# A four-layer convolution and state-space network: every eighth product of the scan on GpSimd, convolutions in quarter tiles, projections as a third metered stream

## The chip, the core and the metric

The kernel runs on one core of one Trainium2 chip. Its time is the device time of one launch in microseconds, the median of several runs. The core's engines work side by side, each through its own list of instructions in order: TensorE (PE in the profile; PEld is its weight load), VectorE (DVE), ScalarE (ACT), GpSimd (POOL) and SyncE (SP), which issues the DMAs. They wait for one another by semaphores.

## The reference

The input `x` is 16 images of 192 channels of 32 x 32, all float32. Four layers follow one another, each as `x = x + layer(_gn(x))`, where `_gn` normalizes groups of channels. Layer 0 is a matrix-LSTM block with a 3x3 convolution and a normalization over the batch. Layer 1 is channel attention between depthwise 3x3 convolutions. Layer 2 is a selective scan in four directions over the 1024 pixels. Layer 3 mixes an image with shifted copies of itself. What matters here is layer 2 and the depthwise convolutions:

```python
def selective_scan(u, delta, A, Bs, Cs, Dskip):
    ...
    def step(h, xs_t):
        d_t, u_t, B_t, C_t = xs_t
        dA = jnp.exp(d_t[..., None] * A)
        h = h * dA + (d_t * u_t)[..., None] * B_t[:, :, None, :]
        y = jnp.einsum('bkdn,bkn->bkd', h, C_t)
        return (h, y)
    ...
xz = jnp.einsum('bchw,oc->bohw', x, in_proj_w)
xx, z = jnp.split(xz, 2, axis=1)
z1 = jax.nn.gelu(z, approximate=False)
xx = jax.lax.conv_general_dilated(xx, conv_w, (1, 1), 'SAME', feature_group_count=D_EXP, ...) + conv_b[None, :, None, None]
xx = jax.nn.gelu(xx, approximate=False)
...
x_dbl = jnp.einsum('bkdl,kcd->bkcl', xs, x_proj_w)
dts, Bs_, Cs_ = jnp.split(x_dbl, [R, R + N], axis=2)
dts = jnp.einsum('bkrl,kdr->bkdl', dts, dt_w)
delta = jax.nn.softplus(dts + dt_b[None, :, :, None])
```

There are 4 directions (K), 384 channels and 16 states (N) per channel, so an image has 4 x 384 x 16 recurrences of 1024 steps.

## The kernel before

**Stages.** `layer0` runs image by image and leaves its results in DRAM. The class `LayersB` does layers 1 to 3. For each image it has three parts. `prepare` (layer 1, and layer 2 up to the gated input `xx`) runs for the image after the one that is being scanned. `scans` does the recurrences. `complete` (the end of layer 2, and layer 3) runs for the image before. So in the long scan stage the scans of image b stand beside `prepare` of b+1 and `complete` of b-1.

**A unit.** A unit is 128 recurrences of 1024 steps: 16 channels by 8 states on the 128 partitions. An image has 192 units (`UNITS`), 48 per direction (`DIR_UNITS`). For unit u the engines do this:

- ScalarE, `decay(u)`: `h[u % 2] = exp(A * dl)`, written to PSUM (L1830).
- GpSimd, `inputs(u)`: `xs[u % 3] = du * bb` in SBUF (L1837), issued two units ahead.
- VectorE, `scan(u)`: one scan instruction in place in `h` (L1844).
- VectorE, `outputs(u)`: `hc[u % 3] = h * cb`, the product with C, written to SBUF (L1849).
- TensorE, `sums(u)`: four matmuls of 32 columns which add `hc` over the states into `acc` (L1882), issued one unit later. After every fourth unit `collect` copies `acc` to `y` on ScalarE (L1892).

SP loads `dl` (ring of two) and `du` (ring of three) for each two units, broadcast from DRAM (L1806), and `bb` and `cb` for each direction (L1800).

**The order by hand.** In the scan stage the order is written out by the program itself. `scans` walks over the units and keeps a model clock for each engine. `prepare` and `complete` are generators, wrapped as a `Stream`; a `yield "PE", 0` tells which engine the next piece uses. After the unit's own instructions `fits` decides whether the next piece of a stream may be issued now: the model clock of its engine must not be further than `OVER` beyond the end of the unit, and `ALLOW` limits what a unit may take on TensorE and VectorE. Costs are metered by `RATES` in `Metered`.

**Projections.** `front(k)` makes the step sizes of a direction: `project` and `steps` on TensorE, `keep`, `ends` and `logs` on ScalarE, `park` on GpSimd, which ends in two stores to DRAM (L1785, L1786). Its pieces have fixed units: `steps` at unit -18, -12, -6, 0, 6 and 12 of the direction, the rest one, two and four units later, whatever the clocks say.

**Convolutions.** `conv` does a depthwise 3x3 convolution on TensorE as nine matmuls with diagonal weights per half of the pixels, 18 in all, each over all channels of the tile (96 or 128). One PSUM bank of the stream holds the sum of a half, and one copy on ScalarE takes it out. `taps` loads the diagonals in three DMAs. For the first image VectorE computes the second half with nine multiply-adds. There are ten convolutions per image.

**PSUM.** `mm` hands out three banks: "bp" for `prepare`, "bc" for `complete`, "bf" for `front`.

**ScalarE's tables.** Exp and Ln lie in one table, Gelu in another. `ln_exp` loads the first explicitly, behind each Gelu and before each Ln; `has_ln` remembers whether it is there.

Most of the streams' instructions carry line L800, that of the metering helper.

Of the kernel before, what the change touches and what calls it, by code (L numbers as in the profile page):

```python
# [41 lines left out]
class Ctx:  # L42


    def __init__(self, tc, cpool, I):
        self.tc, self.nc, self.I = tc, tc.nc, I
        self.ordered = False
        self.has_ln = False
        nc = self.nc
        self.ident = cpool.tile([128, 128], F32, name="ident")  # L50
        nc.sync.dma_start(self.ident, I["c_ident"])
        self.blk6 = cpool.tile([P6, P6], F32, name="blk6")
        nc.sync.dma_start(self.blk6, I["c_blk6"])
        self.eps5 = cpool.tile([128, 1], F32, name="eps5")
        nc.vector.memset(self.eps5, 1e-5)
        self.one = cpool.tile([128, 1], F32, name="one")
        nc.vector.memset(self.one, 1.0)
        self.on192 = cpool.tile([P6, P6], F32, name="on192")
        nc.vector.memset(self.on192, 1.0 / C)
        self.on384 = cpool.tile([128, 128], F32, name="on384")  # L60
        nc.vector.memset(self.on384, 1.0 / INNER)
        self.ones = cpool.tile([128, 128], F32, name="ones")
        nc.vector.memset(self.ones, 1.0)

    def ln_exp(self):

        if self.ordered and self.has_ln:
            return
        self.has_ln = True
        if self.ordered:  # L70
            self.spent["ACT"] += TABLE
        i = self.nc.scalar.preload_act_table_set("natural_log_exp_and_others")
        if not self.ordered:
            self.tc.keep_in_program_order(i)
# [696 lines left out]
SLOT = 3.55  # L771
EARLY = 1.3
OWN = {"POOL": 2.36, "SUMS": 0.6, "START": 0.9, "DECAY": 1.1, "COLLECT": 0.57}
ENGINES = ("PE", "ACT", "POOL", "DVE")
ALLOW = {"PE": 2.7, "DVE": 0.3}
OVER = {"PE": 2.5, "ACT": 1.0, "POOL": 2.5}
LEAST = {"PE": 1.0, "ACT": 0.6, "POOL": 0.8}
# [3 lines left out]

class Metered:


    RATES = {"ACT": (0.07, 0.00105), "POOL": (0.1, 0.0022), "DVE": (0.08, 0.00105), "PE": (0.06, 0.0017)}
    LEAST = {"ACT": 0.2, "POOL": 0.2, "DVE": 0.12, "PE": 0.4}

# [3 lines left out]
    def __getattr__(self, op):  # L791
        f = getattr(self.engine, op)

        def issue(out, *args, **kw):
            base, each = self.RATES[self.name]
            self.spent[self.name] += max(self.LEAST[self.name], base + each * math.prod(out.shape[1:]))
            if op == "activation" and args[1] in (AF.Tanh, AF.Gelu):
                self.spent["ACT"] += TABLE * self.cx.has_ln
                self.cx.has_ln = False
            return f(out, *args, **kw)  # L800

        return issue
# [12 lines left out]
class Stream:  # L815
# [9 lines left out]
    def step(self):  # L825
        self.engine, lag, *mark = next(self.pieces, (None, 0))
        self.ready = self.at + lag
        self.piped = "piped" in mark

# [11 lines left out]
class LayersB:  # L841
# [10 lines left out]
    def mm(self):  # L852

        if self.bank is None:
            self.turn = (self.turn + 1) % 3
            tag = ("bp", "bc", "bf")[self.turn]
        else:
            tag = self.bank
        return self.mmp.tile([128, HL], F32, tag=tag, name="mm")

# [25 lines left out]
    def run(self):  # L886
        tc, NB = self.tc, self.NB
        self.bank, self.turn = None, 0
        with ExitStack() as ctx:
# [11 lines left out]
            self.parked = self.fetched = self.slots = self.scanned = self.read = 0  # L901

# [11 lines left out]
            with tc.manual_schedule():  # L914
                self.before, self.after = Stream(self.all(self.complete), "bc"), Stream(self.all(self.prepare), "bp")
                for b in range(NB):
# [6 lines left out]
    def setup(self):  # L923
# [3 lines left out]
        self.dqd = dp.tile([6, 128, 9, 128], F32, name="dqd")  # L927
        self.dvd = dp.tile([2, 2, P6, 9, P6], F32, name="dvd")
# [168 lines left out]
    def taps(self, p, src, w, first):  # L1097


        d = [self.slot("dg", [p, 3, p], "dg", 3) for _ in range(3)]  # L1100
        tv = None
# [3 lines left out]
        for t in range(3):  # L1105
            three = slice(3 * t, 3 * t + 3)
            if first:
                self.nc.vector.tensor_mul(
                    d[t], self.cx.ident[0:p, 0:p].unsqueeze(1).to_broadcast([p, 3, p]),
                    tv[:, three].unsqueeze(2).to_broadcast([p, 3, p]),  # L1110
                )
                self.nc.sync.dma_start(src[:, three, :], d[t])
            else:
                self.nc.sync.dma_start(d[t], src[:, three, :])
        return d, tv

    def conv(self, out, i, p, taps):


        nc = self.be  # L1120
        d, tv = taps
        for hf in range(2):
            if hf and tv is not None:
                yield "DVE", 0
                o = rows(out[:, half(hf)])
                for t in range(9):
                    v = self.pads[i][0:p, 16 + t // 3 : 32 + t // 3, t % 3 : t % 3 + W]
                    if t == 0:
                        nc.vector.tensor_scalar(o, v, tv[:, 0:1], None, op0=ALU.mult)
                    else:  # L1130
                        nc.vector.scalar_tensor_tensor(
                            o, v, tv[:, t : t + 1], o, op0=ALU.mult, op1=ALU.add
                        )
                continue
            yield "PE", 0
            ps = self.mm()[0:p, :]
            for t in range(9):
                if t in (2, 4, 6):
                    yield "PE", 0
                nc.tensor.matmul(  # L1140
                    ps, lhsT=d[t // 3][:, t % 3, :],
                    rhs=self.pads[i][0:p, 16 * hf + t // 3 : 16 * hf + t // 3 + 16, t % 3 : t % 3 + W],
                    start=(t == 0), stop=(t == 8),
                )
            yield "ACT", 0
            nc.scalar.copy(out[:, half(hf)], ps)

    def prepare(self, b):
# [193 lines left out]
        for g in range(3):  # L1342
            yield "ACT", 0
            nc.scalar.activation(xx[:, g, :], xg[:, g, :], AF.Gelu, bias=self.dw2b[:, g : g + 1])
        cx.ln_exp()
# [7 lines left out]
        for gs in ((0, 1), (2,)):  # L1353
# [10 lines left out]
            for g, z in zip(gs, zs):  # L1364
                yield "ACT", 0
                nc.scalar.activation(z, z, AF.Gelu)
                nc.sync.dma_start(self.zd[one(b), g].rearrange("o p l -> p (o l)"), z)
            cx.ln_exp()
# [5 lines left out]
    def complete(self, b):  # L1374
# [176 lines left out]
        for hf in range(2):  # L1551
# [57 lines left out]
            yield "ACT", 0  # L1609
            nc.scalar.activation(fin, fin, AF.Gelu)  # L1610
            cx.ln_exp()
# [22 lines left out]
    def scans(self, b, more, carry):  # L1634
# [4 lines left out]
        ahead = {}  # L1639
        for d in range(K + more):  # L1640
            for at, piece in self.front(d % K):
                if d % K or (at < 0) == (d > 0):
                    ahead.setdefault(d * DIR_UNITS + at, []).append(piece)
        for t in range(UNITS):
# [3 lines left out]
            for s in (self.before, self.after):  # L1648
                while s.engine == "ACT" and self.fits(s, now + EARLY - OVER["ACT"]):
                    self.advance(s)  # L1650
            if more or t + 1 < UNITS:
                self.decay((t + 1) % UNITS)
                clock["ACT"] += OWN["DECAY"]
# [4 lines left out]
            self.outputs(t)  # L1658
            clock["DVE"] += SLOT
            end = now + SLOT  # L1660
            if t > 0 or carry:
                self.sums((t - 1) % UNITS)
                self.collect((t - 1) % UNITS)
            self.fetch(t, more)
            self.bank = "bf"
            was = dict(self.spent)
            for piece in ahead.pop(t, ()):
                piece()
            for e in ENGINES:
                clock[e] += self.spent[e] - was[e]  # L1670
            for e in ALLOW:
                have[e] = min(have[e], 0.0) + ALLOW[e] - self.spent[e] + was[e]
            if more and t == FETCH:
                while self.parked < b + 2:
                    self.advance(self.after)
                self.fetch_xx()
            if t == UNITS - DIR_UNITS:
                while self.read < b:
                    self.advance(self.before)
            if t == 2:  # L1680
                self.scanned = b
            streams = (self.before, self.after)[:: 1 if t % 2 else -1]
# [6 lines left out]
        if not more:  # L1689
            while self.before.engine:  # L1690
                self.advance(self.before)
# [3 lines left out]
    def fits(self, s, end):  # L1695

        if not s.open(self.slots) or s.engine == "SP":
            return s.engine == "SP" and s.open(self.slots)
        at = self.clock[s.engine]
        if s.engine != "DVE":  # L1700
            end += OVER[s.engine]
        wait = s.inputs()
        if wait > at and (s.engine == "DVE" or wait + LEAST[s.engine] > end):
            return False
        return at < end + 0.1 and self.have.get(s.engine, 1.0) > 0.0

    def advance(self, stream):
        self.bank = stream.bank
        stream.at = self.slots
        was, wait = dict(self.spent), stream.inputs()  # L1710
        stream.step()
        for e in ENGINES:
# [7 lines left out]
    def begin(self):  # L1720

        for at, piece in self.front(0):
            if at < 0:
                piece()
# [12 lines left out]
    def front(self, k):  # L1737


# [48 lines left out]
        out = []  # L1788
        if k % 2 == 0:
            for hf in range(2):  # L1790
                at = -24 + 2 * hf
                out += [(at, lambda hf=hf: project(hf)), (at + 1, lambda hf=hf: keep(hf))]
        for n, at in enumerate((-18, -12, -6, 0, 6, 12)):
            for lag, f in ((0, steps), (1, ends), (2, logs), (4, park)):
                out.append((at + lag, lambda f=f, n=n: f(n // 2, n % 2)))
        return out
# [31 lines left out]
    def decay(self, u):  # L1828
        n, blk = divmod(u, BLOCKS)
        self.nc.scalar.activation(  # L1830
# [8 lines left out]
    def scan(self, u):  # L1839

        h, x = self.h[u % 2], self.xs[u % 3]
        if u // DIR_UNITS >= 2:
            h, x = h[:, ::-1], x[:, ::-1]
        self.nc.vector.tensor_tensor_scan(h, h, x, 0.0, op0=ALU.mult, op1=ALU.add)  # L1844
# [14 lines left out]
    def sums(self, u):  # L1859
# [5 lines left out]
        self.clock["PE"] += OWN["SUMS"]  # L1865
# [132 lines left out]
```

## Time and profile before

| | us |
|---|---|
| runs shown | 15191.56, 15242.16, 15250.05 |
| median | 15242.16 |
| profiled execution | 15228.48 |
| its span, first to last instruction | 15226.7 |

| engine | busy us | share of the span |
|---|---|---|
| TensorE | 12507.7 | 82% |
| VectorE | 12530.6 | 82% |
| ScalarE | 7798.3 | 51% |
| GpSimd | 10305.3 | 68% |

The shares are means over the whole span. The first scan starts at 3311.4 us and the last product ends at about 15091 us, so the scan stage has to be read by itself. In the profile a group of instructions shows its busy time, the mean of one in ns, and the engine's idle time before them with what ended it.

### The profile page before, as it was taken

The page shows a single profiled execution, that of the slowest core. Times are in us where ns is not written, and L with a number is a line of the kernel's source. Part 1 is how long each engine was busy: PE and PEld are TensorE (multiplying, and loading weights), DVE is VectorE, ACT ScalarE, POOL GpSimd, SP SyncE. Part 2 cuts the span into 40 slices and gives each one's busy share as a digit, 9 for nine tenths or more (in the row PEclk, how much of TensorE's full clock was granted, in tenths as well). Part 3 has the DMA queues.
Part 4 walks back from the last instruction along what each step waited for, and adds up shares of the span by engine and source line. Part 5 has one row for each costly group of instructions (what it writes and reads, how often), then busy time and mean ns, then how long its engine had stood idle before and what let it go on. Part 6 is the DMA issues. An engine that isn't in the chain of part 4 may idle for free. (4 is left out here: it accounts for less than half of the span.)

```text
span 15226.7 us, 183204 instructions
## 1 busy us (share of the span) xinstructions
PE 12507.7 (82%) x65856; PEld 4757.9 (31%) x65856; DVE 12530.6 (82%) x10115; ACT 7798.3 (51%) x10376; POOL 10305.3 (68%) x6314
## 2 busy tenths in 40 slices
PE   8999999978787778788887878788887888787655
PEld 4444444422232222222222222222222222222212
DVE  4444444459899999999999899999999999989997
ACT  3333333334555556465646565655555555555554
POOL 2222222227687878787878787878888787878785
PEclk9999999978888888888888888888888878888766
DMA  1000000047778787878777778777777787777775
GB/s 29 15 15 15 15 15 15 15 109 192 202 195 212 188 209 193 209 196 204 195 201 200 195 199 199 202 196 204 196 199 201 203 197 204 193 205 195 198 181 128
DMA packets 884772, 2412.01 MB, mean 158 GB/s; under 512 B 146672, under 2 KB 266944, under 8 KB 876224
## 3 DMA queue, kind: packets, MB, share of 16 engines
q1 hardware_dynamic: 871168, 2397.50, 62.2%
q8 instruction: 532, 8.72, 0.3%
q10 hardware_dynamic: 12736, 3.04, 0.1%
q14 instruction: 336, 2.75, 0.1%
HBM read 2019.10 MB, written 364.30 MB: 157 GB/s over the span
## 5 line engine op out<-in xcount | busy, mean ns | idle before, releaser
L1837 POOL TENSOR_TENSOR xs<-du,bb 128x1024 f32<-128x1024 f32 x3072 | 7236.2, 2365 | 1967.3 <-DVE h L1844 1511.0
L1844 DVE TENSOR_TENSOR_SCAN h<-h,xs 128x1024 f32<-128x1024 f32 x3072 | 7028.1, 2288 | 440.3 <-ACT h L1830 391.4
L1830 ACT ACTIVATE h<-dl,A 128x1024 f32<-128x1024 f32 x3072 | 3424.6, 1116 | 3605.1 <-DVE hc L1849 3066.4
L1882 PE MATMUL acc<-hc,sel 128*32 128x256 f32 x24576 | 2741.8, 527 | 1651.5 <-DVE hc L1849 1640.5
L1849 DVE TENSOR_TENSOR hc<-h,cb 128x1024 f32<-128x1024 f32 x3072 | 3761.9, 1225 | 363.3 <-PE acc L1882 53.0
L800 PE MATMUL mm<-pad,dg 128*128 128x512 f32 (+1 forms) x5580 | 2791.1, 637 | 152.1 <-DMA dg<-dqd 39.0
L627 POOL TENSOR_TENSOR D<-D,mask 128x256 f32<-128x256 f32 x768 | 543.4, 740 | 2100.1 <-DVE D L624 2100.1
L1882 PEld LDWEIGHTS acc<-hc,sel 128*32 128x32 f32 x24576 | 549.8, 118 | 3958.7 <-DVE hc L1849 2717.5
L800 PEld LDWEIGHTS mm<-pad,dg 128*128 128x128 f32 (+1 forms) x5580 | 970.4, 187 | 1682.2 <-issue 1399.8
L800 PE MATMUL mm<-x,wgt 96*128 96x512 f32 (+1 forms) x1664 | 1067.3, 775 | 148.9 <-ACT o L800 43.2
L800 POOL TENSOR_TENSOR t<-x 96x768 f32<-96x768 f32 (+4 forms) x510 | 650.8, 1298 | 79.5 <-ACT x L800 47.8
L800 PE MATMUL mm<-d,xT 128*96 128x256 f32 x2048 | 588.5, 428 | 15.8 <-POOL d L800 13.3
L800 PE MATMUL mm<-xd,dtw 12*128 12x512 f32 x768 | 559.1, 815 | 8.0 <-ACT z L800 8.0
L800 POOL TENSOR_TENSOR duh<-dlh,xx 128x512 f32<-128x512 f32 x384 | 538.3, 1402 | 30.1
L800 POOL TENSOR_TENSOR dlh<-dlh,e 128x512 f32<-128x512 f32 x384 | 488.4, 1272 | 103.7 <-ACT e L800 101.8
L800 PEld LDWEIGHTS mm<-x,wgt 96*128 96x128 f32 (+1 forms) x1664 | 335.4, 223 | 697.1 <-issue 339.9
L391 PE MATMUL pc<-ypad,w_c 128*64 128x512 f32 (+1 forms) x1152 | 480.2, 664 | 74.4 <-PEq L751 41.6
L1892 ACT COPY y<-acc 128x512 f32<-128x512 f32 x384 | 224.6, 585 | 543.3 <-PE acc L1882 539.2
L624 DVE SCALAR_TENSOR_TENSOR D<-D,s 128x256 f32<-128x256 f32 x768 | 271.6, 415 | 255.3 <-ACT D L620 255.3
L1870 PE MATMUL acc<-y,ident 128*128 128x512 f32 x576 | 387.7, 761 | 84.9 <-ACT y L1892 84.9
L800 PEld LDWEIGHTS mm<-d,xT 128*96 128x96 f32 x2048 | 340.2, 179 | 321.2 <-issue 131.6
L620 ACT ACTIVATE D<-s 128x256 f32<-128x256 f32 x768 | 233.3, 389 | 337.9 <-PE s L613 332.4
(321 smaller groups left out, 14230.1 us busy)
## 6 DMA issues: line engine op xcount, KB each, us to landing
dl<-dld SPq DMA_DIRECT2D x1536, 512.0 KB
du<-dud SPq DMA_DIRECT2D x1536, 512.0 KB
dld<-dlh SPq DMA_DIRECT2D x384, 256.0 KB
dud<-duh SPq DMA_DIRECT2D x384, 256.0 KB
bb<-xdr SPq DMA_DIRECT2D x128, 512.0 KB
cb<-xdr SPq DMA_DIRECT2D x128, 512.0 KB
dg<-dqd SPq DMA_DIRECT2D x270, 192.0 KB
zd<-z SPq DMA_DIRECT2D x48, 512.0 KB
```

Source lines behind the costliest of these rows:

```text
L391: nc.tensor.matmul(p[r, :], lhsT=w_, rhs=v, start=(n == 0), stop=(n == 14))
L620: nc.scalar.activation(d, S[j][:, two], AF.Exp)
L624: nc.vector.scalar_tensor_tensor(d, d, 2.0, S[j][:, 2 * CH :], op0=ALU.min, op1=ALU.mult)
L627: nc.gpsimd.tensor_mul(d, d, mask)
L800: return f(out, *args, **kw)
L1830: self.nc.scalar.activation(self.h[u % 2], self.dl[n % 2], AF.Exp, scale=self.A[:, blk, n : n + 1])
L1837: self.nc.gpsimd.tensor_mul(self.xs[u % 3], self.du[n % 3], self.turn_of(self.bb, n // GROUPS, blk))
L1844: self.nc.vector.tensor_tensor_scan(h, h, x, 0.0, op0=ALU.mult, op1=ALU.add)
L1849: self.nc.vector.tensor_mul(self.hc[u % 3], self.h[u % 2], self.turn_of(self.cb, k, at % BLOCKS))
L1870: nc.tensor.matmul(acc, lhsT=self.cx.ident, rhs=self.y[:, g, half(pair)], start=True, stop=False)
L1882: nc.tensor.matmul(self.acc[rows4(q), q4(s)], lhsT=self.sel[:, m, :], rhs=part(q), start=False, stop=(s + m + blk == 3),)
L1892: self.nc.scalar.copy(y, self.acc)
```

## The change

**The product.** For units with `u % 8 == 3` (`pooled`) the scan writes its result to `hc` in SBUF instead of `h` in PSUM, VectorE does no product, and `weigh` does it on GpSimd in place in `hc`. `weigh` is issued one unit later, in front of that unit's `inputs`. The sums of such a unit are issued two units later instead of one. The metering has other limits around a pooled unit (`SOON`). Pieces of the streams for VectorE may now stand between a scan and its product.

**The convolutions.** Channels are split into two blocks of 64 (64 and 32 for tiles of 96) and pixels into two halves: four 64x64 matmuls per tap, over two banks, the stream's own and "bf". A mark "take" keeps other takers of "bf" away until "give". `taps` loads 64 columns of diagonals in one DMA, with two buffers. Four copies on ScalarE take a convolution's result out. The first image's convolutions go the same way.

**The projections.** `front` becomes `fronts` and `ahead`, a generator and third `Stream`, with the same first units, but no fixed lags; `kept` and `ended` force its pieces where a load needs them.

**The tables.** Gelu pieces carry a mark "gelu" and are issued only with room in the unit; `decay` loads the Exp table back itself where Gelu's is there. The explicit loads behind each Gelu are gone.

```diff
-SLOT = 3.55
+SCAN, PRODUCT = 2.29, 1.34
 EARLY = 1.3
-OWN = {"POOL": 2.36, "SUMS": 0.6, "START": 0.9, "DECAY": 1.1, "COLLECT": 0.57}
+OWN = {"POOL": 2.37, "SUMS": 0.8, "TURNED": 1.05, "START": 1.25, "DECAY": 1.12, "COLLECT": 0.59}
+TAP = 1.2
-ALLOW = {"PE": 2.7, "DVE": 0.3}
+ALLOW = {"DVE": 0.45}
 OVER = {"PE": 2.5, "ACT": 1.0, "POOL": 2.5}
+SOON = {"PE": 1.0, "ACT": 0.0, "POOL": 1.0}
+GELU = 1.2
...
+def pooled(u):
+    return u % 8 == 3
...
     def taps(self, p, src, w, first):
-        d = [self.slot("dg", [p, 3, p], "dg", 3) for _ in range(3)]
+        d = self.slot("dg", [p, 9, 64], "dg", 2)
...
-                self.nc.sync.dma_start(d[t], src[:, three, :])
-        return d, tv
+            self.nc.sync.dma_start(d, src)
+        return d
...
+    def conv(self, out, i, p, d):
+        nc = self.nc
+        blocks = [slice(0, 64), slice(64, p)]
+        yield "PE", 0, "take"
+        banks = [self.mm(), self.mm2()]
+        for t in range(9):
+            if t in (2, 4, 6):
+                yield "PE", 0
+            for r, ps in zip(blocks, banks):
+                n = r.stop - r.start
+                for hf in range(2):
+                    nc.tensor.matmul(
+                        ps[64 * hf : 64 * hf + n, :], lhsT=d[r, t, 0:n],
+                        rhs=self.pads[i][r, 16 * hf + t // 3 : 16 * hf + t // 3 + 16, t % 3 : t % 3 + W],
+                        start=(t == 0), stop=(t == 8),
+                    )
+            self.spent["PE"] += TAP
+        for r, ps, mark in zip(blocks, banks, ("", "give")):
+            yield "ACT", 0, mark
+            for hf in range(2):
+                self.be.scalar.copy(out[r, half(hf)], ps[64 * hf : 64 * hf + r.stop - r.start, :])
...
     def scans(self, b, more, carry):
...
+            if t and pooled(t - 1):
+                self.weigh(t - 1)
+                clock["POOL"] += OWN["POOL"]
             if more or t + 2 < UNITS:
                 self.inputs(t + 2)
                 clock["POOL"] += OWN["POOL"]
             self.scan(t)
-            self.outputs(t)
-            clock["DVE"] += SLOT
-            end = now + SLOT
-            if t > 0 or carry:
-                self.sums((t - 1) % UNITS)
-                self.collect((t - 1) % UNITS)
+            clock["DVE"] += SCAN
+            if not pooled(t):
+                for s in (self.before, self.after):
+                    while s.engine == "DVE" and self.fits(s, clock["DVE"]):
+                        self.advance(s)
+                self.outputs(t)
+                clock["DVE"] += PRODUCT
+            end = clock["DVE"]
+            for u in list(owed):
+                if not pooled(u) or u < t - 1:
+                    owed.remove(u)
+                    self.sums(u)
+                    self.collect(u)
+            owed.append(t)
...
     def scan(self, u):
         h, x = self.h[u % 2], self.xs[u % 3]
+        o = self.hc[u % 3] if pooled(u) else h
         if u // DIR_UNITS >= 2:
-            h, x = h[:, ::-1], x[:, ::-1]
-        self.nc.vector.tensor_tensor_scan(h, h, x, 0.0, op0=ALU.mult, op1=ALU.add)
+            h, x, o = h[:, ::-1], x[:, ::-1], o[:, ::-1]
+        self.nc.vector.tensor_tensor_scan(o, h, x, 0.0, op0=ALU.mult, op1=ALU.add)
+
+    def weigh(self, u):
+        k, at = divmod(u, DIR_UNITS)
+        h = self.hc[u % 3]
+        self.nc.gpsimd.tensor_mul(h, h, self.turn_of(self.cb, k, at % BLOCKS))
```

## The prediction

> **What bounds the kernel now.** I read the page first, for the load of each engine and its course over the span.
>
> ```profile
> PE 12507.7 (82%) x65856; PEld 4757.9 (31%) x65856; DVE 12530.6 (82%) x10115; ACT 7798.3 (51%) x10376; POOL 10305.3 (68%) x6314
> DVE  4444444459899999999999899999999999989997
> POOL 2222222227687878787878787878888787878785
> ```
>
> The first fifth (layer 0, up to about 3090 us) isn't touched by the change. The rest is the scan stage, with VectorE (DVE) at nine tenths and GpSimd (POOL) at seven or eight. The steady part of it in one row (busy us of PE, PEld, DVE, ACT, POOL; granted clock; DMA share):
>
> ```profile
> 4000.00:14400.00 10400.00, 8453.72 (x38228) 2889.23 (x38220) 9641.81 (x6316) 5834.95 (x7194) 8447.04 (x4694) 0.83 0.79 200
> ```
>
> The operation counts put 2704 units of 192 per image in it, 14.08 images: 738.5 us per image. The timeline of VectorE shows what a unit costs when nothing is late:
>
> ```profile
> 8007.15 1.22 DVE L1849 TENSOR_TENSOR hc<-h,cb 128x1024 f32<-128x1024 f32 x1
> 8008.29 2.29 DVE L1844 TENSOR_TENSOR_SCAN h<-h,xs 128x1024 f32<-128x1024 f32 x1
> 8010.69 1.22 DVE L1849 TENSOR_TENSOR hc<-h,cb 128x1024 f32<-128x1024 f32 x1
> 8011.83 2.29 DVE L1844 TENSOR_TENSOR_SCAN h<-h,xs 128x1024 f32<-128x1024 f32 x1
> ```
>
> Scan to scan is 3.54 us (3.534 over the next ones), 0.11 of it a gap before the product; 192 of them are 678.5 us. Busy time beyond the units' own 3.424 x 2704 = 9259 is 383 us, 27 per image: norms and adds. The remaining 33 us per image are waits. VectorE's and POOL's waits in the same window (us in total, times, longest):
>
> ```profile
> DVE h L1844 <- ACT h L1830: 357.5, 251, 8.1
> DVE h L1844 <- POOL xs L1837: 5.9, 3, 2.0
> POOL xs L1837 <- DVE h L1844: 1256.1, 981, 7.2
> POOL xs L1837 <- DMA du<-dud: 403.5, 130, 7.3
> ```
>
> So VectorE is the bound, held up now and then by a late decay on ScalarE, hardly ever by POOL. POOL works 8447.0/14.08 = 600 us per image; of its 139 idle us 89 are slack (it waits for the scan), 29 a late `du` load, some 20 other waits. TensorE's 82% isn't a bound: the page has it idle for 1640.5 us in front of the sums, until `hc` is there.
>
> **The product of every eighth unit.** Gone from VectorE: 24 products per image. A unit then costs a scan alone; the next scan depends on nothing in it and starts at its end (2.29) or 0.08 earlier, as scans overlap products above. Saved: 3.534 - 2.25 = 1.28, 24 x 1.28 = 30.7 us per image. VectorE without waits: 678.5 + 27 - 30.7 = 674.8.
> The pooled scan writes `hc` in SBUF instead of `h` in PSUM: no row shows that. The product writes SBUF from the same two kinds of operands in half the time, so the write is no limit: 0, with +-0.1 us (384 x 0.1 = 38 us in all) for the range. It also waits for the sums of three units before, which free `hc`; those are issued a full unit earlier: 0. What would queue behind it is every scan.
> Added to POOL: 24 products, by the nearest row:
>
> ```profile
> L1837 POOL TENSOR_TENSOR xs<-du,bb x3072: 2332/2363/2447, 3309.0 to 15079.3; 128x1024 f32<-128x1024 f32 x192
> L1849 DVE TENSOR_TENSOR hc<-h,cb x3072: 1223/1225/1227, 3313.8 to 15089.9; 128x1024 f32<-128x1024 f32 x192
> L1844 DVE TENSOR_TENSOR_SCAN h<-h,xs x3072: 2249/2289/2299, 3311.4 to 15087.5; 128x1024 f32<-128x1024 f32 x192
> ```
>
> 24 x 2.36 = 56.6 us, so POOL comes to 656.6 per image: 97% of VectorE's waitless 674.8. Here the Trainium skill speaks against the change: "GPSIMD Engine Reference", Engine selection, keeps two-input elementwise work on VectorE, GpSimd being about twice as slow. The rows agree (2.36 to 1.225), and with POOL full, the rule would make it a loss of 24 x (2.36 - 1.28) = 26 us per image, 415 in all. By the waits POOL has 89 us of slack, which holds 56.6; so I take the gain.
> Where the slack is thin: the product stands on POOL in front of the inputs of unit t+3. If POOL enters the short unit L late, it runs inputs, product, inputs and ends at L + 7.1, while scan t+3 starts at 2.29 + 2 x 3.53 = 9.35: up to 2.2 us of lateness cost nothing. But in the changed order (counted with the rows' durations) one of an image's eight stretches of 24 units gives POOL some 5 us more work than VectorE; two are level. That, and fresh waits for `xs`, I put at 7 us per image. POOL's own waits for DMA, ACT and PE (49 per image) bound it from above: 656.6 + 49 = 706, about where VectorE with its waits stands.
>
> **Convolutions.** TensorE rows from the steady window and from layer 0 (by form):
>
> ```profile
> L800 PE MATMUL mm<-pad,dg 128*128 128x512 f32 (+1 forms) x5040 | 2535.0, 639 | 140.9 <-DMA dg<-dqd 37.5 <-ACT v L800 27.3 <-ACT xg L800 20.5
> L391 PE MATMUL pc<-ypad,w_c2p 128*128 128x512 f32 x180 | 88.6, 601 | 0.0
> L391 PE MATMUL pc<-ypad,w_c2p 64*64 64x512 f32 x180 | 41.9, 597 | 0.0
> ```
>
> An f32 matmul is two records. A 64x64 record costs 0.233 us against 0.492, so two run side by side; the four 32-column tiles of the sums start within 20 ns. I take four side by side: a convolution falls from 18 to 9 matmul times, TensorE from 600 to about 510 per image. Bounds: two side by side leaves TensorE as it was; both are hidden, for TensorE waits for VectorE. ScalarE gets 20 more copies per image at 0.584 = 11.7 us. Weights: one 288 KB load where there were three of 192, double-buffered, 320 SP issues and about 36 of 2412 MB less; it takes away at most the 37.5 us (2.7 per image) for which TensorE waited. Taken as 0.
> In the first image VectorE did half of each convolution beside TensorE's half; now TensorE does nine taps of four, in the time of nine: 0, +-20 us over ten convolutions.
>
> **Projections as a metered stream, ScalarE's tables.** Work is unchanged, places move. The stores of `park` reach SP at least one group load before the first load that reads them in 164 of 192 cases for `du` (128 before), so the forced cases become rarer. 540 table loads are in the program instead of 457: 5.2 more per image. The timeline of ScalarE prices one:
>
> ```profile
> 8004.88 1.12 ACT L1830 ACTIVATE h<-dl,A 128x1024 f32<-128x1024 f32 x1 [2.77 <-DVE hc L1849]
> 8006.02 1.28 ACT L800 ACT_TABLE_LOAD   x1
> 8007.31 1.06 ACT L800 ACTIVATE t<-t 96x1024 f32<-96x1024 f32 x1
> ```
>
> The next activation starts 1.29 us behind the load's start. "ScalarE: Activation LUTs", What ACT_TABLE_LOAD costs, gives 2.66 with a drain; the trace shows no drain, and decides: 6.7 us per image, not 13.8. ScalarE goes from 414 to 433 of 715 us. In the unit behind a pooled one its decay has 2.29 us instead of 3.53, so late decays bite harder; but only 17 of the 515 loads among the decays stand there in the changed order. I leave the waits at 33 per image (range 20 to 45).
>
> **Sum.** 674.8 + 33 + 7 = 714.8 per image, 23.7 less. Fourteen middle images: 332. The first has no `complete` beside it (30 saved), the last no `prepare`, but its `complete` is stretched by the fuller POOL (22). Together 384 off the profiled 15228.5: 14844; the median of the runs shown is 14 above it: about 14850 on that footing.
>
> **Rivals.**
> *More than the product* (0.14): fewer waits (forced parks, Gelu tables placed by rule, weights early), 15 instead of 40 per image: 690 to 700, 14500 to 14650. For: 357.5 us of waits on decays. Against: 83 more loads.
> *Eaten* (0.20): POOL's waits now count in full. 725 to 738 per image: 15020 to 15230. For: 97%, and late `du` loads (403.5 us). Against: three `xs` buffers.
> *Slower* (0.20): a full POOL finishes `park` late, SP stands at the `dld` store, the `dl` loads behind it come late, and decay and scan wait. From 82 us of POOL waits per image (656.6 + 82 = 738.5; 49 today) it decides; at 95 the image takes 752, 15430.
> *No overlap of the 64x64 tiles* (within those 0.20): 36 matmuls of 0.86 us per convolution, TensorE at 600 + 155 = 755 per image and thereby the bound: 15470. Two-fold overlap is already shown, so 0.03.
>
> Main case 0.46: 705 to 725 per image, 14700 to 15000. Faster by over 0.5% takes the main case, the first rival and 0.12 of "eaten": 0.72. Within 0.5%, about what a measurement of this kernel can tell from no change, the other 0.08 and 0.02 of "slower": 0.10; slower 0.18. The range takes in the unknown costs, "eaten", most of the first rival and the mild end of "slower": 14600 to 15250.
>
> **What would show it.** Right: 384 POOL rows of `hc<-hc,cb` at 2.36; scans at 2.29 either way; POOL at 91 to 94% in the steady part; VectorE's waits for `xs` up from 5.9 to some 100 us, for decays about as before. Convolution tiles with a busy time near 0.11 us per record. Wrong: pooled scans longer than 2.4; VectorE waits above 65 us per image; SP waiting for `dlh` much over 259 us; TensorE above 90%.

## The result and the profile after

The forecast was faster, 14850 us. The changed kernel is slower: 15827.06 us (15813.14 to 15837.08, 4 runs) beside 15246.1 for the kernel before (15191.56 to 15275.3, 4 runs), a ratio of 1.0385 [1.0354, 1.0415].

The page of the changed kernel shows busy time, course and clock:

```profile
PE 12797.9 (81%) x71796; PEld 4467.7 (28%) x71796; DVE 11983.0 (76%) x9631; ACT 8088.2 (51%) x10789; POOL 11156.2 (70%) x6698
DVE  4444444337888898888888888888788888888997
POOL 2222222226788888888888887979797979798996
PEclk9999999966777786778686768777777777777767
```

VectorE did lose its work: 12530.6 us busy before, 11983.0 now, and 384 products less are 470 us of that. But its share of a slice fell from nine tenths to eight: it waits. The granted clock fell too; on the page before its row was:

```profile
PEclk9999999978888888888888888888888878888766
```

The groups of the changed kernel's page for the new and the moved instructions (busy us and mean ns of one, then idle time before them and what ended it):

```profile
L1907 DVE TENSOR_TENSOR_SCAN h<-h,xs 128x1024 f32<-128x1024 f32 x2688 | 6145.6, 2286 | 602.0 <-ACT h L1892 496.5
L1907 DVE TENSOR_TENSOR_SCAN hc<-h,xs 128x1024 f32<-128x1024 f32 x384 | 875.8, 2281 | 154.4 <-PE acc L1951 118.3
L1918 DVE TENSOR_TENSOR hc<-h,cb 128x1024 f32<-128x1024 f32 x2688 | 3289.2, 1224 | 1059.7 <-PE acc L1951 811.2
L1913 POOL TENSOR_TENSOR hc<-hc,cb 128x1024 f32<-128x1024 f32 x384 | 904.6, 2356 | 290.6 <-DVE hc L1907 287.3
L1899 POOL TENSOR_TENSOR xs<-du,bb 128x1024 f32<-128x1024 f32 x3072 | 7206.9, 2364 | 989.4 <-DVE h L1907 790.9
```

The durations are the forecast ones: pooled scan 2.28 us, GpSimd's product 2.36. GpSimd has 791 us in which it waits for VectorE's scan, so it isn't what is late. New is the wait in front of the products and the pooled scans: both write `hc`, and stand until the sums of three units before have read it (`PE acc L1951`). The waits in the steady part, 4000 to 14900 us (us in total, times, longest):

```profile
DVE hc L1918 <- PE acc L1951: 763.9, 105, 16.3
DVE h L1907 <- ACT h L1892: 438.0, 236, 8.4
DVE hc L1907 <- PE acc L1951: 96.8, 18, 18.5
DVE h L1907 <- POOL xs L1899: 39.6, 38, 1.9
```

The product's wait for the sums in the kernel before, 4000 to 14400 us:

```profile
DVE hc L1849 <- PE acc L1882: 53.0, 40, 3.0
```

Now the two waits for the sums are 860.7 us in 14.19 images (10900 by 768.1 each), 61 per image, in 123 waits. Two of them in the timelines of TensorE and of VectorE:

```profile
5276.90 15.06 PE L1150 MATMUL mm<-pad,dg 64*64 64x512 f32 x32
5291.89 1.08 PE L1951 MATMUL acc<-hc,sel 128*32 128x256 f32 x8
5292.90 11.31 PE L1150 MATMUL mm<-pad,dg 64*64 64x512 f32 x24
5304.14 2.80 PE L1951 MATMUL acc<-hc,sel 128*32 128x256 f32 x24
```

```profile
5280.35 2.30 DVE L1907 TENSOR_TENSOR_SCAN h<-h,xs 128x1024 f32<-128x1024 f32 x1 [1.50 <-POOL xs L1899]
5293.04 1.22 DVE L1918 TENSOR_TENSOR hc<-h,cb 128x1024 f32<-128x1024 f32 x1 [10.39 <-PE acc L1951]
5305.29 1.22 DVE L1918 TENSOR_TENSOR hc<-h,cb 128x1024 f32<-128x1024 f32 x1 [8.83 <-PE acc L1951]
```

This is one convolution of 96 channels. The view cuts off the beginning of its first row: the stretch starts at 5272.36 us and holds three pieces, 48 records in 19.6 us; the fourth piece holds TensorE for 11.3 us. The sums stand behind them in TensorE's list, and VectorE's product comes when the sums have run. In 98 of the 123 waits, 797 of the 860.7 us, records of a 96-channel convolution ran on TensorE during the wait or in the 4 us before it; the other 25 have no convolution there. Windows of the changed kernel, each laid from the first to the last start of a piece, so that what the last records take is left out (length, busy us of PE, PEld, DVE, ACT, POOL, granted clock, DMA share); the records inside tell whether a piece is of a 128- or a 96-channel convolution:

```profile
6141.99:6143.35 1.36, 1.36 (x19) 0.51 (x16) 1.26 (x2) 0.00 (x0) 1.12 (x2) 1.00 1.14 343
6434.23:6437.68 3.45, 3.45 (x19) 0.67 (x16) 3.35 (x3) 1.12 (x1) 2.28 (x2) 1.00 1.03 270
6594.24:6596.88 2.64, 2.63 (x15) 0.80 (x16) 2.54 (x2) 0.97 (x1) 2.56 (x3) 0.50 1.03 234
6009.64:6019.89 10.25, 10.25 (x24) 1.41 (x24) 6.36 (x9) 1.85 (x3) 4.68 (x2) 0.50 0.00 0
```

Rows one and three are two taps (16 records) of a 128-channel convolution, at full and at half clock. Row two is two taps of a 96-channel one at full clock, row four three of its taps (24 records) at half. The starts of the single records in the trace show what differs. In row one, four records start within 0.02 us, and the next four 0.43 us later (0.48 at the beginning of the piece); a record over all channels took the same 0.43 us before, at full clock. A tap is two such groups, 0.86 to 0.91 us. In row two only the two records of one block start together. A tap is four such pairs, 0.45 to 0.53 us apart, 1.98 us in all. At half clock either kind takes about twice as long, and 63% of the 96-channel records start at half clock, but 8% of the 128-channel ones.

Over the whole run a 96-channel tap takes 3.09 us, a 128-channel one 0.97, and a convolution of nine taps 28 and 9 us. Before, each of either kind took 15.5 us at full clock (36 records of 0.43) and some 17 on average. Given as the mean distance from record to record within a piece, the measure of the experiments below, this is 0.374 and 0.106 us. Four of an image's ten convolutions have 96 channels. Their blocks are 64 and 32 channels, so the tiles alternate between 64x64 and 32x32, twice per tap.

Where the 608.6 us between the two spans lie, from the starts of the scans: 120 before the first scan, 95 in the first image, 14 x 29.4 = 411 in the middle ones, -20 in the last, 2 behind it.

### The profile page after: what moved, and what is told of

Read it like the earlier page. It is cut to its first block, busy times and chain, and to the rows that moved or that the text cites. A ratio compares the mean times of both kernels' runs of the same rounds, so it can differ in the third digit from the quotient of the medians.

```text
span 15835.3 us, 193675 instructions
## 1 busy us (share of the span) xinstructions
PE 12797.9 (81%) x71796; PEld 4467.7 (28%) x71796; DVE 11983.0 (76%) x9631; ACT 8088.2 (51%) x10789; POOL 11156.2 (70%) x6698
## 5 line engine op out<-in xcount | busy, mean ns | idle before, releaser
L1907 DVE TENSOR_TENSOR_SCAN h<-h,xs 128x1024 f32<-128x1024 f32 x2688 | 6145.6, 2286 | 602.0 <-ACT h L1892 496.5
L1951 PE MATMUL acc<-hc,sel 128*32 128x256 f32 x24576 | 2791.3, 554 | 1766.9 <-DVE hc L1918 1267.6
L1918 DVE TENSOR_TENSOR hc<-h,cb 128x1024 f32<-128x1024 f32 x2688 | 3289.2, 1224 | 1059.7 <-PE acc L1951 811.2
L1150 PE MATMUL mm<-pad,dg 64*64 64x512 f32 (+1 forms) x11520 | 2683.6, 741 | 73.0 <-ACT pad L813 67.0
L1951 PEld LDWEIGHTS acc<-hc,sel 128*32 128x32 f32 x24576 | 637.3, 126 | 3982.5 <-DVE hc L1918 2155.8
L1913 POOL TENSOR_TENSOR hc<-hc,cb 128x1024 f32<-128x1024 f32 x384 | 904.6, 2356 | 290.6 <-DVE hc L1907 287.3
L1150 PEld LDWEIGHTS mm<-pad,dg 64*64 64x64 f32 (+1 forms) x11520 | 503.3, 143 | 2039.6 <-issue 1869.1
L1907 DVE TENSOR_TENSOR_SCAN hc<-h,xs 128x1024 f32<-128x1024 f32 x384 | 875.8, 2281 | 154.4 <-PE acc L1951 118.3
L813 PE MATMUL mm<-xd,dtw 12*128 12x512 f32 x768 | 609.2, 883 | 278.2 <-ACT xg L813 158.0
L813 PE MATMUL mm<-d,xT 128*96 128x256 f32 x2048 | 643.3, 455 | 44.7 <-POOL d L813 44.7
L1939 PE MATMUL acc<-y,ident 128*128 128x512 f32 x576 | 438.6, 853 | 69.0 <-ACT y L1961 68.6
```

The lines of the kernel that those rows point to most:

```text
L1150: nc.tensor.matmul(ps[64 * hf : 64 * hf + n, :], lhsT=d[r, t, 0:n], rhs=self.pads[i][r, 16 * hf + t // 3 : 16 * hf + t // 3 + 16, t % 3 : ...
L1907: self.nc.vector.tensor_tensor_scan(o, h, x, 0.0, op0=ALU.mult, op1=ALU.add)
L1913: self.nc.gpsimd.tensor_mul(h, h, self.turn_of(self.cb, k, at % BLOCKS))
L1918: self.nc.vector.tensor_mul(self.hc[u % 3], self.h[u % 2], self.turn_of(self.cb, k, at % BLOCKS))
L1939: nc.tensor.matmul(acc, lhsT=self.cx.ident, rhs=self.y[:, g, half(pair)], start=True, stop=False)
L1951: nc.tensor.matmul(self.acc[rows4(q), q4(s)], lhsT=self.sel[:, m, :], rhs=part(q), start=False, stop=(s + m + blk == 3),)
```

## Experiments

Three theories stood at the start. **T**: the tiles of unequal shape in the 96-channel convolutions hold TensorE up, the sums and VectorE behind them; all else in the change does what was forecast. **Rival R**: the product on GpSimd, or the new order of the streams, costs the time itself (its first half is P in the expectations). **M**: the convolutions' pieces are metered too cheaply, whatever the shape of their tiles. All ratios are to the kernel before.

### Equal tiles: `pad64`

The second block of a 96-channel tile is filled up with zero weights to 64x64.

```diff
-        self.dvd = dp.tile([2, 2, P6, 9, 64], F32, name="dvd")
+        self.dvd = dp.tile([2, 2, 128, 9, 64], F32, name="dvd")
...
-        d = self.slot("dg", [p, 9, 64], "dg", 2)
+        d = self.slot("dg", [128, 9, 64], "dg", 2)
...
+            if p < 128:
+                self.nc.vector.memset(d[p:128], 0.0)
...
-                n = r.stop - r.start
+                r = slice(r.start, r.start + 64)
...
-                        ps[64 * hf : 64 * hf + n, :], lhsT=d[r, t, 0:n],
+                        ps[64 * hf : 64 * hf + 64, :], lhsT=d[r, t, :],
```

> The changed kernel with one thing altered: in the four convolutions over 96 channels the second block is padded with zero weights from 32 rows and columns to 64, so that all tiles of all convolutions are 64x64. Theory T (tile shapes: 64x64 and 32x32 tiles alternate in the 96-channel convolutions, don't run side by side and run at half clock; the sums queue behind them and VectorE waits for the sums): their records fall from 0.37 us apart to about 0.11, VectorE's waits for the sums from 70 us per 1000 to under 10, time 14750 to 14950. Rival P (the product on GpSimd holds the sums up, and TensorE behind them): waits and time stay, 15700 to 15850. Rival M (pieces metered at 1.2 us per tap are too many per unit, whatever their shape): 15300 to 15800.

Measured: 14759.81 us, ratio 0.9679 [0.9655, 0.9704]. A record takes 0.104 us on average in all ten convolutions, and 4% of the 96-channel records start at half clock. This version beats both kernels. Two taps of one of its 96-channel convolutions, then its waits and its window from 4000 to 14000 us:

```profile
6060.19:6061.55 1.36, 1.36 (x19) 0.51 (x16) 1.36 (x2) 0.73 (x1) 1.36 (x1) 1.00 1.00 290
```

```profile
DVE h L1909 <- ACT h L1894: 398.9, 240, 8.6
DVE h L1909 <- POOL xs L1901: 55.5, 57, 1.9
DVE hc L1920 <- PE acc L1953: 15.3, 22, 2.2
```

```profile
4000.00:14000.00 10000.00, 7504.66 (x43331) 2506.95 (x43330) 9244.52 (x6000) 6063.15 (x7538) 9228.31 (x5047) 0.79 0.80 206
```

The wait for the sums is all but gone, 1 us per image of 707.6. More multiplications, the same order of instructions, 1067 us less: the shape of the tiles is the cause of the loss. The order of the streams, R's second half, is not, and with equal tiles the same metering does no harm.

### Fewer changes of shape: `order96`

In the 96-channel convolutions all taps of a piece go first to block 0, then to block 1: 8 changes of block per convolution instead of 18.

```diff
-        for t in range(9):
-            if t in (2, 4, 6):
+        for ts in ((0, 1), (2, 3), (4, 5), (6, 7, 8)):
+            if ts[0]:
                 yield "PE", 0
-            for r, ps in zip(blocks, banks):
+            for r, t, ps in [(r, t, ps) for r, ps in zip(blocks, banks) for t in ts] if p < 128 else [
+                (r, t, ps) for t in ts for r, ps in zip(blocks, banks)
+            ]:
...
-            self.spent["PE"] += TAP
+            self.spent["PE"] += TAP * len(ts)
```

> The changed kernel with 64x64 and 32x32 tiles as they are, but in the 96-channel convolutions all taps of a piece are done for the first block and then for the second: 8 changes of tile shape per convolution instead of 18. If the change of shape is what costs (a gap of about 0.14 us at each, and nothing overlaps across it): records 0.25 to 0.30 us apart instead of 0.37, time 15400 to 15700. If the shape alone costs (two tiles side by side at most, clock at half): 0.35 to 0.37 apart and 15750 to 15900.

Measured: 15550.4 us, ratio 1.0195 [1.0177, 1.0213]; 0.331 us per record, between the two expectations. Two taps at full clock and three at half, windows as above:

```profile
6390.82:6394.01 3.19, 3.19 (x20) 0.83 (x16) 3.09 (x3) 1.12 (x1) 2.02 (x2) 1.00 1.03 266
6011.06:6020.64 9.58, 9.58 (x27) 2.12 (x24) 3.43 (x2) 2.17 (x3) 5.38 (x4) 0.50 0.07 7
```

Two changes fewer save 0.26 us (3.45 to 3.19), 0.13 each. Two taps of unequal tiles lose 2.09 us against the 128-channel ones (3.45 less 1.36). Three changes are 0.39 of them. The rest is that the records start in pairs where they started in fours: four more steps of 0.43 us, 1.72. The sum, 2.11, is the loss. "TensorEngine Tiling (Array Packing)" in the Trainium skill has a rule for this under Key Properties: changing the tiling mode drains TensorE, while the tiles of one mode run in parallel. The starts of the records agree, as no record of one block starts beside one of the other; a drain itself is not seen in the trace, and the page names no price. The prediction didn't hold this rule against the 64 and 32.

### Rows equal, columns not: `rows64`

As `pad64`, but the second block has 64 rows and 32 columns.

```diff
...
-        d = self.slot("dg", [p, 9, 64], "dg", 2)
+        d = self.slot("dg", [128, 9, 64], "dg", 2)
...
                 n = r.stop - r.start
+                r = slice(r.start, r.start + 64)
```

> As the version with padding to 64x64, but only the rows of the second block are padded: its tiles have 64 rows and 32 columns. If rows decide whether tiles of the two blocks run side by side: records 0.11 to 0.13 us apart, time 14750 to 14850. If any difference in shape breaks it: 0.3 us and more apart, 15500 to 15850.

Measured: 15293.17 us, ratio 1.003 [1.0018, 1.0042]. A record of a 96-channel convolution takes 0.276 us; neither expectation holds. Two taps at full clock:

```profile
6223.60:6227.05 3.45, 3.45 (x20) 0.67 (x16) 3.35 (x3) 1.12 (x1) 2.28 (x2) 1.00 1.03 252
```

That is 3.45 again: at full clock a second block of 64x32 costs just what one of 32x32 costs: a difference in columns alone ends the overlap too. The mean is lower than with 32x32 (0.276 to 0.374) because fewer of these records start at half clock, 17% instead of 63%. As tiles and order cost the same at full clock, the clock is all that is left to set this run 534 us below the changed kernel (15827.06 less 15293.17), half of what `pad64` regains. Why the clock is granted more often here, the runs don't show.

The waits for the sums follow what a tap takes. `order96` first, then `rows64`, 4000 to 14000 us:

```profile
DVE hc L1920 <- PE acc L1953: 560.2, 91, 15.3
DVE hc L1909 <- PE acc L1953: 71.3, 15, 14.4
DVE hc L1921 <- PE acc L1954: 366.9, 89, 14.6
DVE hc L1910 <- PE acc L1954: 45.2, 18, 8.3
```

With a mean 96-channel tap of 3.09 us (the changed kernel), 2.78 (`order96`), 2.29 (`rows64`) and 0.94 (`pad64`), an image holds 61, 48, 30 and 1 us of them.

### Without the pooled product: `nopool` and `pad64_nopool`

```diff
 def pooled(u):
-    return u % 8 == 3
+    return False
```

In `nopool` this stands alone, in `pad64_nopool` beside the equal tiles.

> The changed kernel without the pooled units: every product is on VectorE again; convolutions and streams as changed. Theory T: the waits for the sums stay, VectorE gets 30 us per image of work back: 15900 to 16200. Rival P: waits for the sums go, 15150 to 15350.

> The kernel with all convolution tiles at 64x64 (second block of the 96-channel ones padded), without pooled units: every product on VectorE. It gives the product's worth where TensorE is in time, and the worth of convolutions and streams alone against the kernel before. Theory T, with the prediction's sum of 30.7 us per image less 7: 15100 to 15300, so 370 to 500 above the version with pooled units. Rival P: the product gives nothing, 14750 to 14900.

Measured: `nopool` 16220.34 us, 1.0639 [1.0603, 1.0676]; `pad64_nopool` 15126.99 us, 0.9919 [0.9903, 0.9936]. R's first half falls: taking the product away makes it slower both times (`nopool` is 20 us above the range expected under T). Between the two kernels with equal tiles it is worth 15126.99 - 14759.81 = 367 us, 728.4 - 707.6 = 20.8 per image where 23.7 was forecast. Convolutions and streams without it bring 0.8%.

### The product alone: `pool_only` and `pool_room`

The kernel before with the pooled product and its sums one unit later, and nothing else. The part of the edit that moves the model clock:

```diff
...
-            self.outputs(t)
-            clock["DVE"] += SLOT
-            end = now + SLOT
+            if not pooled(t):
+                self.outputs(t)
+            clock["DVE"] += 2.29 if pooled(t) else SLOT
+            end = clock["DVE"]
...
```

`pool_room` is the same with `SLOT = 3.75` instead of 3.55.

> The kernel before with the product of every eighth unit on GpSimd and the sums of these units one unit later; convolutions, projections and tables as before. Theory T with the prediction's sum: VectorE 30.7 us per image less, its waits up by 5 to 15: 14800 to 15050. Rival P: POOL late, projections and loads behind it late, 15250 to 15600.

> pool_only (the kernel before with the product of every eighth unit on GpSimd) with a model unit of 3.75 us instead of 3.55, so that the model clocks of POOL and TensorE leave the streams the room per image that they have in before (685 us of model time against 682). T: pool_only's loss came from streams that the shorter model units starved; now the product saves 20 to 24 us per image, 14850 to 14950, ratio 0.973 to 0.981. If GpSimd can't carry the products beside the stores and loads of before's projections (the prediction's own slower rival), 15250 to 15500 with waits of VectorE for xs or for late dl loads.

Measured: `pool_only` 17389.81 us, 1.1407 [1.1388, 1.1426], a miss; `pool_room` 15018.53 us, 0.9848 [0.9831, 0.9864]. In `pool_only` images 0 to 3 take 705 to 728 us, then they grow to 970. The model unit is shorter there: 168 x 3.55 + 24 x 2.29 = 651 us per image, and GpSimd's own work in it is 216 x 2.36 = 510 and the streams' some 147 (600 less 192 x 2.36): 657. The streams fall behind and are forced in long blocks:

```profile
DVE hc L1858 <- ACT h L1843: 525.4, 26, 80.9
DVE x L805 <- PE mm L805: 442.0, 42, 58.8
```

With room in the model the product saves 12.7 us per image (738.7 to 726.0), not 20 to 24; the expectation was missed by some 70 us. What takes the rest are decays:

```profile
DVE h L1858 <- ACT h L1843: 501.8, 307, 5.8
DVE h L1858 <- POOL xs L1850: 50.6, 71, 3.6
```

501.8 us in 13.77 images are 36 per image, where the kernel before has 25. The changed kernel, with its own limits around a pooled unit, has 31, `pad64` 28. So the re-metering probably has a part in the gain: the two savings differ by 8 us per image (20.8 less 12.7). No run changes those limits alone.

### The convolutions alone: `conv128` and `conv128_room`

The changed kernel with the convolutions of before: 18 matmuls over all channels, one bank, weights in three loads. In `conv128` a matmul is metered at 1.03 us, in `conv128_room`, shown here, at 0.6:

```diff
...
+                self.nc.tensor.matmul(
+                    ps, lhsT=d[t // 3][:, t % 3, :],
+                    rhs=self.pads[i][0:p, 16 * hf + t // 3 : 16 * hf + t // 3 + 16, t % 3 : t % 3 + W],
+                    start=(t == 0), stop=(t == 8),
+                )
+                self.spent["PE"] += 0.6
...
```

> The changed kernel with the convolutions of before (18 matmuls over all channels, one bank, three loads of diagonals; all on TensorE in the first image too), metered at 1.03 us a matmul; product on GpSimd and streams as changed. Theory T: VectorE's waits for the sums fall below 15 us per 1000, time 14800 to 15050. Rival P: 15600 to 15850. Rival M: between, as TensorE has more work than with 64x64 tiles but is metered at its true cost: 14850 to 15100.

> The convolutions of before (18 matmuls of all channels, one bank) in the changed kernel, as in conv128, but metered at 0.6 us per matmul, so that the streams get as much room for them as they get for the tiles (10.8 us per convolution). T (the harm of the change sits in its 96-channel convolutions alone; the four-fold tiles are worth little because TensorE has room): a convolution takes 15.5 us again instead of 7.6 or 26.9, and the time comes near that of pad64, 14750 to 15000, ratio 0.967 to 0.985. If the quarter tiles carry the gain of pad64 themselves, 15200 or more. If the streams starve again, images of over 900 us behind forced pieces, and the run says nothing about either.

Measured: `conv128` 22540.82 us, 1.4781 [1.4743, 1.4818]; `conv128_room` 15300.42 us, 1.0034 [1.0022, 1.0047]. Both miss, and neither is a clean answer, since `prepare` in the first and `complete` in the second get no room and are forced. In the second, 181 of the 534 us by which its span exceeds that of `pad64` lie in scan-to-scan distances over 8 us, most at unit 144, where `complete` must have read its input, and 106 behind the last scan. By its number this run falls where the expectation put quarter tiles that carry the gain themselves. Images 3 to 6, ahead of the first such block, speak against it: they take 715 us on average (703 to 723), those of `pad64` 709. That is too much scatter to put a price on the quarter tiles, and their worth stays open.

### Metering at the true price: `meter96` and `pad64_tap`

```diff
-            self.spent["PE"] += TAP
+            self.spent["PE"] += TAP if p == 128 else 3.0
```

`meter96` meters the slow tiles at about what a tap of them takes (3.09 us); `pad64_tap` is `pad64` with `TAP = 0.9`, near the 0.94 to 0.97 us that its taps take.

> The changed kernel with the 96-channel convolutions metered at 3.0 us per tap instead of 1.2; the same instructions in another order. Theory T: the slow tiles stay at 0.37 us a record, but fewer stand ahead of the sums; VectorE's waits for the sums fall by half or more, time 15000 to 15400. Rival P: unchanged, 15750 to 15900. Rival M: the cause is wholly in the metering, so this alone brings 14750 to 14950.

> pad64 with a tap metered at 0.9 us instead of 1.2, which is nearer to its measured 0.85 and gives TensorE's pieces of the streams more room. T: TensorE is not the limit in pad64 (its sums hold VectorE up for 15 us in 10000), so 14700 to 14800, ratio to before 0.964 to 0.971, no difference to pad64 beyond 0.3%. If the metering of TensorE still holds the streams back, faster than pad64 by 0.5% or more.

Measured: `meter96` 22024.11 us, 1.4447 [1.441, 1.4483]; `pad64_tap` 15228.23 us, 0.9987 [0.998, 0.9994]. Both miss. In `meter96` the honest price leaves `prepare` no room in the units and it is forced as one chain, 1262 us per image. The waits for the sums did fall, to 46.9 us in 10000, so the price does keep the pieces from in front of them; with tiles this slow the loss only moves to `prepare`. In `pad64_tap` a lower price on TensorE makes the kernel 468 us slower than `pad64`. Its waits from 4000 to 14000 us hold the new ones:

```profile
DVE h L1909 <- ACT h L1894: 332.3, 228, 7.4
DVE x L813 <- PE mm L813: 161.9, 27, 18.2
DVE yh L813 <- PE mm L813: 151.0, 12, 38.7
```

The longest distances between scans, up to 64 us, stand at unit 144 of images 6 to 15, and the tail behind the last scan is 245 us instead of 139: `complete` comes late there. Why cheaper taps let it fall behind was not settled; a greedy order can get worse when a piece gets shorter. The 14759.81 of `pad64` is thus also a matter of an order that happens to fit.

## Why the prediction was wrong

**The step that failed** is the convolution: "I take four side by side: a convolution falls from 18 to 9 matmul times, TensorE from 600 to about 510 per image. Bounds: two side by side leaves TensorE as it was; both are hidden, for TensorE waits for VectorE." It failed in three places.

*The shape.* Four side by side holds for the six 128-channel convolutions (0.97 us per tap). In the four 96-channel ones the records run in pairs, which was the worse of its two bounds, and 18 changes of shape at 0.13 us come on top, for which it had no term: 17.8 us per convolution at full clock (9 x 1.98), against 15.5 before. The second block of 32 was in view; it was costed as if it were 64.

*The clock.* It had no term for it either. With 63% of these records at half clock a 96-channel convolution takes 28 us on average, above what both ends of the bounds allowed.

*"Hidden".* TensorE's total never bound anything: 8606.26 us busy in 10900 are 79%, its sum of work would have fitted. What counts is the stretch between two groups of sums. The three pieces at 5272 us were metered at six taps of 1.2, 7.2 us, and took 19.6; TensorE runs its list in order, and the sums stand behind them. `hc` has three buffers, and a stretch that outlasts them stops VectorE. TensorE's 1640.5 us in front of the sums before were slack in units of a few us, no store for stretches of 11 and more.

**What held.** By the steps of the sum, with `pad64` as the change without its fault: VectorE without waits 674.8 us per image forecast, and waits of 33 for decays and others and 7 for `xs`; measured are 28 for decays, 4 for `xs`, 1 for the sums and 3 others, and 674.8 + 36 = 711 stands beside 707.6. The pooled scan into SBUF cost nothing (2.28 us). GpSimd's share of the steady part was to be 91 to 94%: 9228.31 of 10000 in `pad64` (in the changed kernel itself 85%). Its waits don't count in full: it carries the product without becoming the bound, and the rule on two-input work on VectorE, weighed there, was rightly left aside. In the changed kernel itself the waits for decays are 31 and for `xs` 3 per image; 4 others and 61 for the sums come on top, 98 before rounding, and 674.8 + 98 = 773 stands beside 768.1.

**The first image** was put at 0 +-20: it is +120 before its scans and +95 in them. VectorE builds the diagonals into two buffers there and waits for TensorE to free them (changed kernel, 3000 to 4200 us):

```profile
DVE dg L1127 <- PE mm L1150: 209.1, 8, 41.1
```

"TensorE does nine taps of four, in the time of nine" is the same error. In `pad64` the wait for the diagonals' buffers is 113.9 us, and this part is 17 before the scans and -21 in them, within the range given.

**The rivals.** The one on the slower side named a late `park`. SP did wait longer for it (807.9 us for `dlh` from 4000 to 14000, 256.2 before), yet the waits for decays rose only from 25 to 31 us per image, and `pad64` has 931.1 us of the same wait, 28 for decays, and is faster: that sign came and was no sign. "No overlap of the 64x64 tiles" was nearest to what happened, but priced as TensorE's sum of work for all ten convolutions, and set at 0.03 since "two-fold overlap is already shown". The rows that showed it were of one shape. Of the signs that would speak against the forecast, the other that came is VectorE's waits above 65 us per image (98). Of those for it, the waits for `xs` stayed far below the 100 us named: 39.6, and 55.5 in `pad64`.

## What to carry to other kernels

When matmuls are packed as tiles, look at the smallest tensor that goes through the same code. In this kernel tiles that follow one another had to have one shape, and filling up with zeros was cheaper than an odd rest. Work on an engine with idle time is hidden only if each stretch of it between two pieces of the urgent work is shorter than the slack of the buffers behind it; compare the longest stretch with the ring, not the sum with the span. Where a program orders its instructions by a model, a cost that is changed there is a change of its own, and an experiment that moves it has to be read for forced work first.

## What the hardware showed

- Four 64x64 tiles over two banks run fully side by side: four records start within 0.02 us and the next four 0.43 us later at full clock, the time of one record over 128 rows and columns before. Alternating with 32x32 or with 64x32 tiles, they start in pairs, and two taps take 3.45 us from first to last start instead of 1.36, for either shape; with two changes less 3.19.
- The granted clock in the 96-channel pieces was often 0.50 with TensorE busy all the time, also with no DMA in the window (10.25 us at 0.50, DMA share 0.00). Of the records of the 96-channel convolutions 63% started at half clock with 32x32 tiles between, 17% with 64x32, and 4% when all were 64x64. The mean clock of a run was 0.78 with the unequal tiles of the changed kernel, 0.82 with the equal ones of `pad64`, 0.845 before. What lowers it is not shown.
- A scan with its result in SBUF and one with its result in PSUM take the same time, 2281 and 2286 ns.
